# A four-layer image kernel: the last layers on other engines, the circuit made first, fewer stages ahead of the first scan steps

## The chip, the cores and the metric

The kernel runs on one core of one Trainium2 chip. A core has five engines that take their own instructions in order and wait for each other through semaphores: PE (TensorE, matmuls; its weight loads are listed as PEld), DVE (VectorE), ACT (ScalarE, table functions), POOL (GpSimd) and SP (SyncE, which here only sends DMAs). The metric is the device time of one launch in microseconds (us), the median of three runs.

## What is computed

Thirty-two images of 128 channels and 32 x 32 pixels, all in fp32, go through four layers, each added to its input after a group norm over groups of four channels:

```
x = x + conv3x3(gn(x))                       # layer 0
x = x + vmamba(gn(x))                        # layer 1: four scan directions an image
x = x + coord_attention(gn(x))               # layer 2: two scans, along rows and columns
x = x + quantum(gn(x))                       # layer 3: a 4-qubit circuit a pixel
```

The scans of layers 1 and 2 are state space models with 256 channels and 16 states: per step `h = exp(dt*A)*h + dt*u*B`, `y = sum(h*C)`. Layer 2 turns its scans into four maps an image of 32 values a channel, one of which belongs to rows and one to columns in each product:

```
result_h = sigmoid(a_h) * x_y          # rows by columns
result_w = sigmoid(a_w) * x_x          # columns by rows
out = gn(x) * conv1x1(concat(result_h, result_w))
```

Layer 3 maps each pixel to four angles (a 1x1 convolution), puts them into the state of four qubits, applies two rounds of fixed gates, measures four values and maps these to 128 channels.

## The kernel before

**Layers 0 and 1 (`images`, L873).** For each image four directions are scanned. A direction has 32 steps (two halves of channels, 16 states), each on tiles of 128 channels by 1024 pixels. Step `i` has a decay `da` on ACT (L610), an input `bu` from PE that DVE multiplies (L646, or PE transposes in 11 of 32 steps), the scan on DVE (L654), a product with `cc` on POOL (L663) and a sum in PSUM on PE (L683). `cc` is loaded by SP from `rows` in DRAM (L602), three steps ahead. 4096 such steps run one after another.

What prepares a direction is a list of small stages: `stages` (L243) has eight projections with a Silu (L263, L723), two `small` products (L282), the store of `rows`, two transposes, and the eight stages of `rates(0)`. `rates(h)` (L342) makes dt and du of one half in eight stages: `rate`, `expo`, `rounded`, `log` on PE and ACT, and then `lost`, two `whole` and `weighed` on POOL. `turns(h)` (L404) makes two transposes of du.

`Plan` (L478) puts these stages beside the scan steps by hand-written costs: a stream has a first step, a last step by which it must be done, and its stages are issued as credit on the engines allows. `Plan.alone` (L523) issues all waiting stages at once, with no scan step beside them. All this stands in a `manual_schedule` block (L1058): the order in the program is the order on each engine. Before the first step the block runs alone: layer 0 of the first image, all of the first direction's stages, transposes and second rates, and ten stages of the second direction.

**Layer 2 (`attention`, L1089)** runs two directions of 32 steps over all images together, with the same classes (`Mamba`, `Direction`, `Steps`). Its decays are also cleared at each row's start on POOL (L613). Before its first step it runs alone (L1191): the first direction's stages and both of its rates, and then ten stages of the second direction. Ahead of that it calls `circuit` (L1217), which makes from the weights of layer 3 what the last part needs: `wt` and `wb` (sixteen angle combinations), `ut` (what the circuit does to 16 sines) and `wz` (from 32 squares to 128 channels). `circuit` is some 180 small instructions on DVE with three small matmuls on PE and one sine on ACT. It stands outside the `manual_schedule` block, where the order on each engine is chosen by a scheduler that simulates the engines, oldest work first.

**The last part (`tail`, L1315)**, also ordered by the scheduler, takes one image after another: the rest of layer 2, and layer 3. For each image SP loads `xt` from DRAM (L1329). DVE makes the outer products `rh` and `rw` of the maps (L1333, L1334), PE multiplies them with `adj` (L1340, L1341), DVE normalizes `xt` (L771), multiplies by the matmul's result (L1342) and adds to `xt` (L1343). `group_stats` (L748) takes mean and variance with two small matmuls, the root on ACT (L766) and the reciprocal on DVE (L767); DVE normalizes (L771). For each half of 512 pixels a matmul `q_ps` gives 16 angles in turns (L1353), DVE takes off the whole turns in three instructions (L1354 to L1356, with `MAGIC` added and subtracted), ACT makes one sine of 16 x 1024 (L1359), PE multiplies by `ut` (L1363), ACT squares (L1364), PE multiplies by `wz` (L1368), and DVE adds the result and a bias to `xt` (L1369). POOL sends the DMA of the output (L1372). The pool `img` has three buffers for each name, so three images are on the way at most; `xn` is used twice an image.

PSUM buffers come from `mm` (two buffers) and, in the last part, `adj` and `q` (three each).

Of the kernel before, what the change touches and what calls it, by code (L numbers as in the profile page):

```python
# [43 lines left out]
def constants():  # L44
# [16 lines left out]
    small = np.zeros((16, 16 + 1 + 16 + 32))  # L61
    small[:NQ, 0:16] = turns
    small[:, 16:17] = offset
    small[:, 17:33] = start
    small[:NQ, 33:65] = ez
# [99 lines left out]
class Work:  # L165
# [10 lines left out]
    def tile(self, shape, dtype, tag, name):  # L176
        return self.pool.tile(shape, dtype, tag=tag, name=name, bufs=self.BUFS.get(tag, 1))

# [527 lines left out]
class Kernel:  # L706
# [120 lines left out]
    def run(self):  # L827
        tc, nc, d = self.tc, self.nc, self.d
        with ExitStack() as ctx:
# [25 lines left out]
            with ExitStack() as scans:  # L855
# [9 lines left out]
                self.attention(right)  # L865
# [7 lines left out]
    def images(self):  # L873
        tc, nc, d = self.tc, self.nc, self.d
        with ExitStack() as ctx:
# [182 lines left out]
            with tc.manual_schedule():  # L1058
                w = ways[0]
                plan.add(  # L1060
                    layer0(images[0]) + w.stages() + w.turns(0) + w.rates(1) + w.turns(1)
                    + ways[1].stages()[:10], 0, 0,
                )
                plan.alone()
                each = Steps.SLOTS
                for k, w in enumerate(ways):
# [12 lines left out]
                    if k + 1 < len(ways):  # L1079

                        done, b = 0 if k else 10, ways[k + 1]
                        plan.add(b.stages(at)[done:] + b.turns(0), at - 14, at + each)
                        plan.add(b.rates(1, at + 19) + b.turns(1), at + 19, at + each + 11)
# [5 lines left out]
    def attention(self, right):  # L1089
# [4 lines left out]
        with ExitStack() as ctx:  # L1094
# [13 lines left out]
            self.circuit(right, par)  # L1108
# [78 lines left out]
            with tc.manual_schedule():  # L1187
                each = Steps.SLOTS
                plan = Plan(self)
                ahead = ways[1].stages()  # L1190
                done = 5 * T // ch  # L1191
                plan.add(ways[0].stages() + ways[0].rates(1) + ahead[:done], 0, 0)
                plan.alone()
                for a, w in enumerate(ways):
# [3 lines left out]
                plan.add(ahead[done:], 1, each - 4)  # L1198
# [18 lines left out]
    def circuit(self, keep, pool):  # L1217
        nc, d = self.nc, self.d
        small = keep.tile([16, 65], F32, name="csmall")
        nc.sync.dma_start(small, d["csmall"])  # L1220
        signs, offset, start, ez = small[:NQ, 0:16], small[:, 16:17], small[:, 17:33], small[:NQ, 33:65]
# [6 lines left out]
        qw = pool.tile([16, 2 * NQ, 3], F32, name="qw")  # L1228
        nc.sync.dma_start(qw.rearrange("p a b -> p (a b)"), d["qw"].to_broadcast([16, 24]))


        self.wt = keep.tile([P, 16], F32, name="wt")
        ps = self.mm()
        nc.tensor.matmul(ps[:, :16], pre, signs, start=True, stop=True)
        nc.vector.tensor_copy(self.wt, ps[:, :16])
        self.wb = keep.tile([16, 1], F32, name="wb")
# [156 lines left out]
```

## Time and profile before

| what | us |
|---|---|
| median of three runs | 15466.06 |
| the three runs | 15443.43, 15467.32, 15466.06 |
| the profiled execution | 15464.45 |
| its span, first to last instruction | 15462.6 |
| first scan step starts | 133.65 |
| last step of layer 1 starts its scan | 14536.69 |
| first scan step of layer 2 starts | 14637.53 |
| first product of the last part starts | 14887.67 |
| mean granted clock of PE (share of full speed) | 0.915 |

The page sums all stages. Four fifths or more of the span are busy on each of PE, DVE, ACT and POOL, and nearly all of that is the 4096 steps of layer 1. The last part is 575 us, 3.7% of the span; there the engines stand quite differently, as the page's second part shows at a glance:

```profile
DVE  5888988898898889888898888989898888989787
ACT  6788888888888888888888888888888888888632
POOL 5888888888888888888888888888888888888730
PEclk8899999999999999999999999999999999999877
```

Each digit is the busy share of a fortieth of the span (387 us) in tenths, and in the last row the granted clock of PE in tenths of full speed. The last part fills the last digit and half of the one before it: POOL is nearly idle there, and PE's clock is lower.

### The profile page before, as it was taken

How to read it: one execution, taken by the hardware profiler on the slowest of the kernel's cores; microseconds unless marked ns; L12 is line 12 of the kernel's file. 1: busy time of each engine (PE TensorE's matmuls, PEld its weight loads, DVE VectorE, ACT ScalarE, POOL GpSimd, SP SyncE). 2: the span in 40 equal slices, each digit the busy share in tenths (PEclk: the TensorE clock that was granted, in tenths of full speed). 3: DMA queues.
4: the chain of work that ended last, by engine and by line, in shares of the span. 5: the costliest groups of instructions: out<-in, count | busy, mean ns of one | idle time of the engine just before them, and what ended most of it. 6: DMA issues, size and time to landing. Idle time of an engine off the chain costs nothing.

```text
span 15462.6 us, 197603 instructions
## 1 busy us (share of the span) xinstructions
PE 13209.3 (85%) x70318; PEld 8520.9 (55%) x70318; DVE 13557.1 (88%) x8999; ACT 12314.9 (80%) x21242; POOL 12569.5 (81%) x6433
## 2 busy tenths in 40 slices
PE   7888888888888888888888888888888888888776
PEld 4555555555555555555555555555555555555431
DVE  5888988898898889888898888989898888989787
ACT  6788888888888888888888888888888888888632
POOL 5888888888888888888888888888888888888730
PEclk8899999999999999999999999999999999999877
DMA  3444444444444444444444444444444444444321
GB/s 108 145 147 152 155 152 152 156 155 151 151 156 152 151 155 156 154 151 154 151 156 152 153 151 151 155 152 155 153 157 151 151 153 152 155 151 157 130 96 57
DMA packets 633029, 2277.43 MB, mean 147 GB/s; under 512 B 76808, under 2 KB 80280, under 8 KB 631912
## 3 DMA queue, kind: packets, MB, share of 16 engines
q1 hardware_dynamic: 625128, 2246.09, 42.8%
q0 software_dynamic: 4608, 16.78, 0.3%
q8 instruction: 555, 9.09, 0.2%
q14 instruction: 434, 3.56, 0.1%
q10 hardware_dynamic: 2304, 1.90, 0.0%
HBM read 2221.24 MB, written 43.25 MB: 146 GB/s over the span
## 4 chain that ended last, share of the span: by engine, by line
PE 33%; ACT 27%; DVE 22%; issue 11%; POOL 6%; DMA 1%; DVEq 0%; SPq 0%; POOLq 0%; ACTq 0%
DVE hh L654 15%; ACT da L610 8%; ACT but L639 7%; PE y L683 7%; DVE bu L646 6%; PE mm L263 6%; PE bu L624 3%; PE bu L630 3%; POOL hh L663 3%; PE mm L925 3%; PE y L679 3%; ACT L729 2%; POOL du L394 2%; PE mm L977 2%; PE mm L360 2%
## 5 line engine op out<-in xcount | busy, mean ns | idle before, releaser
L663 POOL TENSOR_TENSOR hh<-hh,cc 128x1024 f32<-128x1024 f32 x4160 | 9784.8, 2365 | 2102.5 <-DVE hh L654 1039.2
L654 DVE TENSOR_TENSOR_SCAN hh<-da,bu 128x1024 f32<-128x1024 f32 x4160 | 9413.8, 2279 | 527.6 <-PE bu L624 176.1
L610 ACT ACTIVATE da<-dt,m_na 128x1024 f32<-128x1024 f32 x4096 | 4610.1, 1143 | 591.3 <-DVE hh L654 488.9
L683 PEld LDWEIGHTS y<-cbig,hh 128*128 128x128 f32 x33280 | 3996.5, 148 | 1635.4 <-issue 1120.5
L683 PE MATMUL y<-cbig,hh 128*128 128x128 f32 x33280 | 4655.0, 286 | 147.9 <-POOL hh L663 144.3
L646 DVE TENSOR_TENSOR bu<-du,bu 128x1024 f32<-128x1024 f32 x2752 | 3330.7, 1210 | 714.2 <-PE bu L630 704.7
L639 ACT ACTIVATE but<-dut,bt 128x128 f32<-128x128 f32 x11264 | 3432.5, 391 | 0.0
L630 PE MATMUL bu<-parts,sel 48*128 48x512 bf16 x5504 | 1719.0, 394 | 649.1 <-DVE hh L654 608.2
L263 PE MATMUL mm<-hpad,m_wc 128*128 128x512 f32 x4096 | 2107.9, 639 | 2.9 <-DVE sz L446 0.8
L624 PE MATMUL bu<-cbig,but 128*128 128x128 f32 x11264 | 1639.3, 294 | 430.9 <-DVE hh L654 395.8
L624 PEld LDWEIGHTS bu<-cbig,but 128*128 128x128 f32 x11264 | 1400.5, 153 | 534.0 <-issue 321.0
L263 PEld LDWEIGHTS mm<-hpad,m_wc 128*128 128x128 f32 x4096 | 732.4, 198 | 849.5 <-issue 784.8
L679 PE MATMUL y<-m_skip,uc 128*128 128x128 f32 x4096 | 658.0, 327 | 383.1 <-ACT back L703 232.9
L630 PEld LDWEIGHTS <-sel 48*128 48x128 bf16 x5504 | 317.7, 94 | 1167.5 <-DVE hh L654 668.1
L679 PEld LDWEIGHTS y<-m_skip,uc 128*128 128x128 f32 x4096 | 613.9, 235 | 527.4 <-ACT back L703 287.6
L723 ACT ACTIVATE uc<-mm,m_pv 128x512 f32<-128x512 f32 x512 | 343.8, 686 | 377.5 <-PE mm L263 372.8
L385 POOL TENSOR_TENSOR w<-w,du 128x1024 f32<-128x1024 f32 x260 | 614.1, 2362 | 29.7 <-ACT w L378 29.7
L422 ACT COPY dut<-mm 128x512 f32<-128x512 f32 x512 | 296.5, 579 | 428.0 <-PE mm L417 425.2
L723 ACT ACT_TABLE_LOAD x482 | 618.4, 1283 | 8.6
L729 ACT ACT_TABLE_LOAD x482 | 618.4, 1283 | 8.5
L389 POOL TENSOR_TENSOR dt<-dt,relu 128x1024 f32<-128x1024 f32 x260 | 615.2, 2366 | 0.0
L394 POOL TENSOR_TENSOR du<-dt,uc 128x1024 f32<-128x1024 f32 x260 | 614.6, 2364 | 0.3
(227 smaller groups left out, 10734.5 us busy)
## 6 DMA issues: line engine op xcount, KB each, us to landing
cc<-rows SPq DMA_DIRECT2D x4160, 512.0 KB, 3.7
xt<-in_x SPq DMA_DIRECT2D x32, 512.0 KB, 4.3
x<-xt SPq DMA_DIRECT2D x32, 512.0 KB, 3.7
xt<-x SPq DMA_DIRECT2D x32, 512.0 KB, 3.5
out<-xt POOLq DMA_DIRECT2D x32, 512.0 KB, 2.9
rows<-dbl SPq DMA_DIRECT2D x130, 64.0 KB, 3.6
stats<-st SPq DMA_DIRECT2D x32, 36.0 KB, 2.3
means<-stats SPq DMA_DIRECT2D x1, 1152.0 KB, 6.3
```

Of the source, the lines that this page charges most:

```text
L263: nc.tensor.matmul(self.view(ps), m.wc[:, v, j, h * P : (h + 1) * P], self.taps(j, c), start=(j == 0), stop=(j == 3),)
L610: k.nc.scalar.activation(t, w.dt[h], AF.Exp, scale=w.m.na[:, h, n : n + 1])
L624: k.nc.tensor.matmul(t[:, b * P : (b + 1) * P], but[:, b], k.ident, start=True, stop=True, is_transpose=True,)
L630: k.nc.tensor.matmul(t[:, cs], k.sel[:, n], w.parts[:, cs], start=True, stop=True)
L639: k.nc.scalar.activation(t[:, b], w.dut[h][:, b], AF.Copy, scale=w.bt[:, b, n : n + 1])
L646: k.nc.vector.tensor_tensor(t, w.du[h], t, ALU.mult)
L654: k.nc.vector.tensor_tensor_scan(way(t), way(self.da.pop(i)), way(self.bu.pop(i)), 0.0, ALU.mult, ALU.add)
L663: k.nc.gpsimd.tensor_tensor(t, t, self.cc.pop(i), ALU.mult)
L679: nc.tensor.matmul(self.y[g][: w.bl, b], w.uc[h][:, at], m.skip[:, h], start=(b == 0), stop=False)
L683: nc.tensor.matmul(self.y[g][: w.bl, b], t[:, at], k.ident, start=False, stop=(n == DS - 1 and b == w.per - 1), is_transpose=True,)
L723: self.nc.scalar.activation(*args, AF.Silu, **kw)
L729: self.nc.scalar.preload_act_table_set("natural_log_exp_and_others")
```

## The change

The diff has four parts.

1. *The last part.* The outer products, the sum into `xt` and the root (as a power of -0.5 of variance plus 1e-5) go to POOL. Both normalizations go to ACT as `scale * x + bias`. The angles of the two halves of 512 pixels are put side by side: the first half's 16 at partitions 0 to 15, the second's at 32 to 47, so that the three steps of the sine, the sine and the Square run once on 64 partitions of 512 columns instead of on two halves or on 16 x 1024.
2. *The circuit* is made after layer 0 of the first image, inside the `manual_schedule` block, in slices of the `carry` buffer, with its values on 64 partitions instead of 16. Its four results go to DRAM and are loaded again at the start of the last part.
3. *Layer 1's first step.* Ahead of it are now issued alone the first direction's stages, its first transposes, and four of the eight stages of its second rates. The other four, the second transposes and the whole of the second direction's stages come beside the first steps.
4. *Layer 2's first step.* The same: ahead of it come the first direction's stages, eight stages of the second direction, and four stages of the second rates; the rest comes beside the first steps.

```diff
-                plan.add(
-                    layer0(images[0]) + w.stages() + w.turns(0) + w.rates(1) + w.turns(1)
-                    + ways[1].stages()[:10], 0, 0,
-                )
+                plan.add(layer0(images[0]), 0, 0)
                 plan.alone()
+                self.circuit(Slices(self.work.tile([P, 2 * HW], F32, tag="carry", name="small")))
+
+                rates = w.rates(1)
+                done = 4
+                plan.add(w.stages() + w.turns(0) + rates[:done], 0, 0)
+                plan.alone()
+                plan.add(rates[done:] + w.turns(1), 0, 11)
...
-                        done, b = 0 if k else 10, ways[k + 1]
-                        plan.add(b.stages(at)[done:] + b.turns(0), at - 14, at + each)
+                        b = ways[k + 1]
+                        plan.add(b.stages(at) + b.turns(0), at - 14, at + each)
...
-                ahead = ways[1].stages()
-                done = 5 * T // ch
-                plan.add(ways[0].stages() + ways[0].rates(1) + ahead[:done], 0, 0)
+                rates = ways[0].rates(1)
+                done = 4
+                ahead, begun = ways[1].stages(), 4 * len(chunks)
+                plan.add(ways[0].stages() + ahead[:begun] + rates[:done], 0, 0)
                 plan.alone()
+                plan.add(rates[done:], 0, 12)
...
-                plan.add(ahead[done:], 1, each - 4)
+                plan.add(ahead[begun:], 1, each - 2)
...
+        self.saved = {}
+        for name in ("wt", "wb", "wz", "ut"):
+            made = getattr(self, name)
+            self.saved[name] = self.dram.tile(list(made.shape), F32, name=name, bufs=1)
+            nc.sync.dma_start(self.saved[name], made)
...
+            mr = par.tile([P, self.n], F32, name="mr")
+            nc.vector.scalar_tensor_tensor(
+                mr, self.means[:, :, 2 * L], -1.0, self.means[:, :, 2 * L + 1], ALU.mult, ALU.mult
+            )
...
-                nc.vector.tensor_tensor(grid(rh), rows(sah), cols(xy), ALU.mult)
-                nc.vector.tensor_tensor(grid(rw), cols(saw), rows(xx), ALU.mult)
+                nc.gpsimd.tensor_tensor(grid(rh), rows(sah), cols(xy), ALU.mult)
+                nc.gpsimd.tensor_tensor(grid(rw), cols(saw), rows(xx), ALU.mult)
...
-                self.normalize(xn, xt, self.means[:, i, 2 * L :])
+                nc.scalar.activation(
+                    xn, xt, AF.Identity, bias=mr[:, i : i + 1],
+                    scale=self.means[:, i, 2 * L + 1 : 2 * L + 2],
+                )
...
-                nc.vector.tensor_tensor(xt, xt, xn, ALU.add)
-                mv = self.group_stats(xt, img)
+                nc.gpsimd.tensor_tensor(xt, xt, xn, ALU.add)
...
+                nc.vector.tensor_scalar(dv, ps[:, 0:1], 1e-5, None, ALU.add)
+                nc.gpsimd.tensor_tensor(mv[:, 1:2], dv, self.power, ALU.pow)
+                nc.vector.scalar_tensor_tensor(
+                    mv[:, 0:1], mv[:, 0:1], -1.0, mv[:, 1:2], ALU.mult, ALU.mult
+                )
...
-                self.normalize(xn, xt, mv)
...
+                nc.scalar.activation(xn, xt, AF.Identity, bias=mv[:, 0:1], scale=mv[:, 1:2])
+                kk = img.tile([64, 512], F32, tag="kk", name="kk")
+                rr = img.tile([64, 512], F32, tag="rr", name="rr")
+                sq = img.tile([64, 512], F32, tag="sq", name="sq")
+                ps = psl.tile([P, 512], F32, tag="q", name="q_ps")
+                for at, cs in halves:
+                    nc.tensor.matmul(
+                        ps[at : at + 32], wt[:, at : at + 32], xn[:, cs], start=True, stop=True
+                    )
+                nc.vector.tensor_scalar(kk, ps[:64], wb, MAGIC, ALU.add, ALU.add)
+                nc.vector.tensor_scalar(kk, kk, MAGIC, None, ALU.subtract)
+                nc.vector.scalar_tensor_tensor(rr, ps[:64], wb, kk, ALU.add, ALU.subtract)
                 nc.scalar.activation(rr, rr, AF.Sin, scale=TWO_PI)
...
+                ps = psl.tile([P, 512], F32, tag="q", name="psi_ps")
+                for at, _ in halves:
+                    nc.tensor.matmul(
+                        ps[at : at + 32], ut[at : at + 32], rr[at : at + 32], start=True, stop=True
+                    )
+                nc.scalar.activation(sq, ps[:64], AF.Square)
+                for at, cs in halves:
                     ps = psl.tile([P, 512], F32, tag="q", name="out_ps")
...
+                    nc.tensor.matmul(
+                        ps, wz[at : at + 32], sq[at : at + 32], start=True, stop=True
+                    )
```

`halves` is `[(0, first 512 columns), (32, last 512 columns)]`; `self.power` is a column of -0.5.

## The prediction

> **What bounds the kernel now.** I read the page first, then the busy time by stage, then one image of the last part in order of time, then the first 140 us and the stretch around 14600 us.
>
> ```profile
> PE 13209.3 (85%) x70318; PEld 8520.9 (55%) x70318; DVE 13557.1 (88%) x8999; ACT 12314.9 (80%) x21242; POOL 12569.5 (81%) x6433
> ```
> ```profile
> 140.00:14541.00 14401.00, 12474.97 (x68386) 8225.49 (x68384) 12858.27 (x7904) 11926.53 (x20798) 12322.59 (x6211) 0.93 0.45 153
> 14888.00:15380.00 492.00, 343.66 (x695) 105.04 (x695) 380.66 (x634) 141.77 (x169) 14.91 (x28) 0.80 0.17 61
> ```
> ```profile
> 15141.00:15158.07 17.07, 11.86 (x24) 3.58 (x24) 13.10 (x22) 5.06 (x6) 0.54 (x2) 0.80 0.18 63
> ```
>
> Columns of the stages: PE, weight loads, DVE, ACT, POOL busy, granted clock, DMA share, GB/s. The 14401 us of scan steps are not edited; only what stands ahead of them and after them moves. In the last part POOL works 15 of 492 us. One image takes 17.07 us there, 13.10 of them DVE. What holds DVE in the other 4 us is seen in one image, in order of time:
>
> ```profile
> 15141.68 1.28 ACT L766 ACT_TABLE_LOAD   x1 [3.31 <-PE mm L765]
> ...
> 15143.27 0.16 DVE L767 RECIPROCAL gn_mv<-gn_dv 128x1 f32<-128x1 f32 x1 [2.31 <-ACT gn_dv L766]
> ...
> 15144.34 3.25 PE L1353 MATMUL q_ps<-xn,wt 128*16 128x512 f32 x4 [2.74 <-DVE xn L771]
> ...
> 15147.62 0.74 DVE L1354 TENSOR_SCALAR kk<-q_ps,wb 16x512 f32<-16x512 f32 x1 [0.63 <-PE q_ps L1353]
> ...
> 15150.43 1.28 ACT L1359 ACT_TABLE_LOAD   x1 [7.19 <-DVE rr L1356]
> ...
> 15150.88 1.21 DVE L1333 TENSOR_TENSOR rh<-maps 128x1024 f32<-128x1024 f32 x1
> ...
> 15151.53 0.19 PEld L1341 LDWEIGHTS adj_ps<-rw,adj 128*128 128x128 f32 x1 [0.24 <-issue]
> 15151.96 1.02 PE L1341 MATMUL adj_ps<-rw,adj 128*128 128x512 f32 x2
> ```
>
> The brackets are idle time and what ended it: 2.31 us behind a square root that first loads its table, 0.63 and 0.54 us (the first kk) behind a matmul at half clock. Passes of 512 columns start 0.43 us apart in `adj_ps`, 0.86 apart in `q_ps`. Ahead of the scans:
>
> ```profile
> 99.73 1.13 ACT L382 ACTIVATE dt<-du,one 128x1024 f32<-128x1024 f32 x1
> ```
> ```profile
> 133.65 2.29 DVE L654 TENSOR_TENSOR_SCAN hh<-da,bu 128x1024 f32<-128x1024 f32 x1 [1.32 <-ACT da L610]
> ```
> ```profile
> 14614.83 15.84 PE L263 MATMUL mm<-means,my_wc 128*128 128x512 f32 x32 [8.01 <-ACT relu L369]
> ```
> ```profile
> 14598.10 0.42 POOL L314 TENSOR_TENSOR rest<-bt,three 128x128 f32<-128x128 f32 x1
> ```
>
> The first scan needs the decays of dt[0]; it starts 32.8 us after the last of the ACT steps that the change keeps ahead of it (100.86).
>
> [...]a switch of set costs a load[...]: 1.28 us, twice per image, for the root and the sine; the Square after the sine loads nothing. [...]L314 reads two operands as eight short rows and takes 0.42 us, less than 128 elements in proportion to the 2.36 us of 1024; so eight breaks cost nothing there. An operand with step 0, as the outer products have, no run shows.[...]
>
> **The last part, per image.**
> DVE: two products (0.69 + 0.67), statistics 1.27 + 0.20, small steps 0.15 + 0.16 + 0.22, add eps 0.16 and the new bias 0.22 (as L819 and L763), kk 0.74, subtract 0.41, rr 0.73, output 2 x 0.75: 7.1 us against 13.1. The sine's three steps run once on 64 partitions, at the price of one on 16 (512 columns either way).
> POOL: three tensor_tensors at 2.41 us (starts 83.17, 85.58, 88.00 at L389 and L394), the power 0.56 (L820), the output's DMA issue 0.53: 8.3 us against 0.5. This takes step 0 as free; bounds: 2.36 us each, as dense[...]. I take the first, because of L314.
> ACT: two normalizings at 1.24 (L912), sine 0.6 (as the Square of 512 columns), Square 0.59: 3.7 us, no table load after the first.
> PE: 8 adj, 4 q, 4 psi, 4 out passes as before, 20 x 0.43 = 8.6, plus two statistics of 0.38: 9.4 us at full clock. Half clock throughout gives 18. If q, psi and out each run their halves at once, 6 passes fall away: 6.8. I take 9.4.
> The ring of three `xt` buffers: load 3.5 (its row in the DMA table), normalizing 1.25, products 1.35, sum 2.4, statistics 1.5, PE and DVE to the variance 2.1, power 0.65, bias 0.2, normalizing 1.3, q 1.8, kk to rr 1.85, sine 0.7, psi 1.85, Square 0.65, out and its adds 2.7, issue 0.5, landing 2.9 (DMA table): 27.2 us, a third is 9.1.
> So nothing is below 9.4. Before, the image took 1.30 times its bound (17.07 / 13.10); without the root's wait of 2.31 it would be 1.13. That gives 10.6 to 12.2; I take **11.0 us**: 31 intervals x (17.07 - 11.0) = **-188 us**. Bounds 9.2 and 14.
> Added waits: the power stands in POOL's in-order queue, where a product of 2.4 us for a later image may be ahead of it, and the output's issue holds the products behind it until `xt` is final; both are in the 11.0. Five loads ahead of the first `xt` on SP (adj, wt, wb, wz, ut) put it 1.3 us later (0.33 each), hidden under the first products. After the last q the old order takes 22 us (15440.62 to 15462.6), the new about 19: q 3.6, DVE 1.85, sine 0.6, psi 3.6, Square 0.6, out 3.8 + 0.75, issue and landing 3.4 to 5.3: **-3**.
>
> **The circuit moved to the front.** Its three matmuls stand on PE between the first image's `inner` and the first projection; the second waits for the buffer that ACT frees at 50.35, so the projections start about 51.2 instead of 48.7: **+2.5 us**. The angles' sine adds a table load and a wait on ACT, over at about 54.8, where the first Silu's input is ready. DVE's 22 us of gates (14568.8 to 14592.5) end near 76; DVE is idle until the first scan, which hides them. SP sends wt, wb, wz and ut to DRAM in order, so `rows` (67.74 before) and the first `cc` wait for ut, to 77 and 79, landing by 85, and POOL needs them after the first scan. The `carry` buffer is first needed 16 steps into the scans. At 14571.0 the circuit's matmuls stood before `g8`, 1.4 us of PE with csmall's landing in front: **-1.7 us**.
>
> **Shorter ways.** In the images ACT's log of the second half ends at 100.86 + 2.5 = 103.4, the first decay at 104.5, the scan starts at 104.6 instead of 133.65: -29.0. Four POOL steps (9.6 us), two transposes and ten stages of the next direction now lie beside the first 32 steps, which took 104.9 us (32 scans counted from 133.6 to 238.5). In the next three directions, with such stages and more, 32 scans took 115.2, 124.6 and 113.8 us (the last ones bear a whole next image); over all, 32 steps take 14401 / 128 = 112.5 us. I take 110: +5. Bounds 0 and +11. Net with the circuit's delay counted: **-24**.
> In the attention PE sat idle for 8.01 us before `my_wc`. Now these projections follow the first rates: two chunks 14603.6 to 14610.5, then Silu after the log (14610.5) and a table load, two more to 14619.5, the second rates with their own table load to 14628.1, first decay 14629.2, scan 14629.5 against 14637.53: -8.0. The left-over POOL steps and two `small` stages cost about 2 in steps that run at 3.51 us on DVE (2.29 + 1.21): **-6**, with the circuit's -1.7 **-7.5**; bounds -4 and -10.
>
> **Sum.** -188 - 3 - 24 - 7.5 = -222.5 against the profiled execution's 15464.45 us (span 15462.6): 15242. The median of three runs, 15466.06, is 1.6 higher: **15244 us**.
>
> **Rivals.**
> A, the forecast, images of 10 to 12.5 us: 15213 to 15290; 50%.
> B, PE's halves overlap and the ring is the bound, 9.2 us: -244 - 34.5, 15187. For it: 6 of 20 passes[...]. Against it: 17 dependent hops between five in-order engines. 18%.
> C, the order on POOL becomes the bound: products of later images stand before the sum and the power of the older one[...]. At 13.65 us: -106 - 34.5, 15325. 27%.
> D, slower than before: step 0 makes POOL read row by row.[...] It is slower as soon as the image takes over 17.07 + 34.5 / 31 = 18.2 us, a product about 7.3 us. L314 speaks against it. 3%.
> E, images bounded by something unseen at nearly the old pace, so that the gain at the front is all: about 15435; 2%.
>
> **How the numbers follow.** A whole, half of B and half of C give 15180 to 15345, which holds about 8 in 10. A run can tell a change of about 0.2%, 31 us. A, B and C are faster by more than that: 0.95; E is no change: 0.02; D: 0.03.
>
> **What would show it.** Right: image intervals near 11 us in `xt` stores; no ACT_TABLE_LOAD between images; `rh` and `rw` on POOL at 2.4 us; DVE busy 7 of 11; first scan near 105, the attention's near 14604 (14637.5 less 24, 8 and 1.7); PEclk above 0.9 in the last part. Wrong: POOL rows for `rh` above 2.6 us; POOL idle before `rh` released by the output's adds (C); q passes 0.86 apart; a first 32 steps of 116 us or more.

## The result and the profile after

| | before | after | predicted |
|---|---|---|---|
| median, us | 15466.69 (4 runs) | 15379.16 (4 runs, 15378.28 to 15380.64) | 15244 (15180 to 15345) |
| profiled execution | 15464.45 | 15378.86 | 15242 |
| first scan step starts | 133.65 | 101.77 | 104.6 |
| first seven directions (224 steps) | 822.5 | 805.5 | 827.5 |
| other steps of layer 1, order of instructions unchanged | 13580.5 | 13572.3 | no change |
| last scan of layer 1 to first of layer 2 | 100.85 | 90.48 | 91.2 |
| 64 steps of layer 2 | 230.0 | 230.2 | 232 |
| last scan to the end (the last part) | 595.1 | 576.7 | 404 |
| granted clock of PE, whole span | 0.915 | 0.911 | |

The ratio of after to before is 0.9946 (95% interval 0.9929 to 0.9963): faster by 0.5%, not by the 1.4% that I forecast. The stages sum to -31.9 - 17.0 - 8.2 - 10.4 + 0.2 - 18.4 = -85.7 us, the difference of the two profiled executions (-85.6). The front (-31.9 - 17.0 - 10.4 + 0.2) gave -59, where the prediction had -31.5; 22 of the 28 us that it gave beyond this lie in the first seven directions. The -8.2 lies in steps whose order did not change. Of the 191 us expected in the last part, 18 came.

The page's first line, the same stages, and one image of the last part, after the change (columns as in the prediction):

```profile
PE 13201.1 (86%) x70318; PEld 8521.4 (55%) x70318; DVE 13366.8 (87%) x8776; ACT 12274.3 (80%) x21181; POOL 12786.4 (83%) x6561
```
```profile
105.00:14484.00 14379.00, 12511.47 (x68439) 8243.13 (x68438) 12857.62 (x7906) 11942.52 (x20818) 12334.36 (x6215) 0.92 0.45 153
14821.00:15300.00 479.00, 319.89 (x672) 97.04 (x672) 182.53 (x413) 99.53 (x111) 216.00 (x146) 0.70 0.17 61
15054.00:15071.07 17.07, 11.50 (x25) 3.42 (x24) 6.59 (x15) 3.59 (x4) 7.25 (x6) 0.70 0.16 61
```

The work moved as forecast: per image DVE fell from 13.10 to 6.59 us, POOL rose from 0.54 to 7.25, ACT fell from 5.06 to 3.59, and table loads in the last part fell from 64 to 1. Yet an image still takes 17.07 us, and now no engine is busy for more than 11.5 of them. Output stores begin 17.07 us apart in both kernels: the 25 intervals in the middle sum to 426.7 us before and 424.9 after. What differs is mainly the last three (60.9 and 39.5 in sum).

So one has to look for a loop of waits instead of a busy engine. Three of the longest in the view of waits of the last part (window 14900 to 15300; total us, times, longest):

```profile
POOL rh L1373 <- PE adj_ps L1382: 170.3, 24, 7.1
DVE gn_st L1388 <- POOL xt L1385: 116.5, 24, 4.9
ACT xn L1406 <- DVE gn_mv L1402: 115.0, 23, 5.0
```

Each of these comes once per image and lasts 5 to 7 us. One image in order of time, with the links that carry the loop:

```profile
15057.75 0.21 DVE L1390 BATCH_NORM_AGGREGATE gn_ag<-gn_st 128x2 f32<-128x12 f32 x1
15057.79 1.13 PE L1427 MATMUL out_ps<-sq,wz 32*128 32x512 f32 x4
...
15058.85 0.38 PE L1392 MATMUL mm<-gn_ag,cbig 128*128 128x1 f32 x2
...
15061.60 0.56 POOL L1401 TENSOR_TENSOR gn_mv<-gn_dv,power 128x1 f32<-128x1 f32 x1
15062.20 0.16 DVE L1402 SCALAR_TENSOR_TENSOR gn_mv<-gn_mv 128x1 f32<-128x1 f32 x1 [0.69 <-POOL gn_mv L1401]
15062.45 1.24 ACT L1406 ACTIVATE xn<-xt,gn_mv 128x1024 f32<-128x1024 f32 x1 [5.00 <-DVE gn_mv L1402]
...
15063.74 1.92 PE L1412 MATMUL q_ps<-xn,wt 128*32 128x512 f32 x4 [2.43 <-ACT xn L1406]
...
15065.71 0.74 DVE L1415 TENSOR_SCALAR kk<-q_ps,wb 64x512 f32<-64x512 f32 x1 [3.36 <-PE q_ps L1412]
15066.38 0.67 DVE L1384 TENSOR_TENSOR xn<-xn,adj_ps 128x512 f32<-128x512 f32 x1
...
15067.10 2.08 PE L1382 MATMUL adj_ps<-rh,adj 128*128 128x512 f32 x2 [1.44 <-DVE xn L1384]
...
15069.26 1.91 POOL L1373 TENSOR_TENSOR rh<-maps 128x1024 f32<-128x1024 f32 x1 [7.10 <-PE adj_ps L1382]
...
15071.13 2.33 POOL L1385 TENSOR_TENSOR xt<-xt,xn 128x1024 f32<-128x1024 f32 x1
```

Read on from the root of image i (L1401): its second normalizing (L1406), its angles `q_ps`, its `kk`, and only then, behind `kk` in DVE's queue, the multiply of image i+1 (L1384). The multiply frees a PSUM buffer for an `adj` matmul of a later image, that one frees the buffer into which POOL writes a product `rh`, and the sum of image i+1 (L1385) stands behind this product on POOL. After it come that image's statistics, mean, variance, root: the loop is closed, once per image. Little of it overlaps with the next image, because each queue holds the next image's instruction behind this image's.

The first three lines, one image earlier, show that a second path runs beside this one and is a little longer. The statistics are done at 15057.96 (`gn_ag`), but the mean (L1392) starts only at 15058.85, when PE is through with `out` (L1427). So the path over POOL has 0.9 us to spare, and the mean waits for PE's queue; what stands in it is seen below, in the experiment that moves the sum.

At the front the mechanism is the forecast one. The last log and the first decay now stand right ahead of the first scan, and the projections `my_wc` start at 14543.5 instead of 14614.8 (57 us of that from the earlier end of layer 1):

```profile
99.56 1.13 ACT L399 ACTIVATE dt<-du,one 128x1024 f32<-128x1024 f32 x1
100.60 5.29 ACT L627 ACTIVATE da<-dt,m_na 128x1024 f32<-128x1024 f32 x5
101.77 2.29 DVE L671 TENSOR_TENSOR_SCAN hh<-da,bu 128x1024 f32<-128x1024 f32 x1 [4.50 <-ACT da L627]
```
```profile
14543.51 16.29 PE L280 MATMUL mm<-means,my_wc 128*128 128x512 f32 x32
```

### The profile page after: what moved, and what is told of

It reads as the page before. It is cut to its first block, busy times and chain, and to the rows that moved or that the text cites. A ratio compares the mean times of both kernels' runs of the same rounds, so it can differ in the third digit from the quotient of the medians.

```text
span 15377.0 us, 197657 instructions
## 1 busy us (share of the span) xinstructions
PE 13201.1 (86%) x70318; PEld 8521.4 (55%) x70318; DVE 13366.8 (87%) x8776; ACT 12274.3 (80%) x21181; POOL 12786.4 (83%) x6561
## 5 line engine op out<-in xcount | busy, mean ns | idle before, releaser
L406 POOL TENSOR_TENSOR dt<-dt,w 128x1024 f32<-128x1024 f32 x260 | 615.3, 2367 | 0.2
```

What stands on the lines that cost most here:

```text
L406: nc.gpsimd.tensor_tensor(self.dt[h], self.dt[h], t[name], op)
```

## The experiments

"Interval" is the time between the starts of two output stores in the middle of the last part; "tail" runs from the last scan to the end. Eight of the changed kernels ran once, and not all on the same chip; the kernel before took 15435 to 15467 us beside them (medians, the lowest a single run). The tail is a better measure than the total: the unchanged steps of layer 1 vary from 13541 to 13581 us between the profiles. The tail varies too: nearly the same last part took 595.1 and 602.4 us in the first two rows. In the traces of the kernels before and after PE's clock is granted at full or at half speed, and each of the 862 and 872 stretches at one of these, but for the last, which the end of the trace cuts off, lasts a whole multiple of 3.413 us (1 to 29 of them; in the kernel after, 15004.92 to 15011.75 is at 1.00 and 15011.75 to 15021.99 at 0.50); these 3.413 us are the window of PE's clock that the texts below count in.

| kernel | total, us | tail | interval | clock in the tail |
|---|---|---|---|---|
| before | 15466.69 | 595.1 | 17.07 | 0.78 |
| front alone | 15404.77 | 602.4 | 17.07 to 18.07 | 0.76 |
| front, root on POOL | 15414.27 | 605.5 | 17.24 to 18.69 | 0.69 |
| after | 15379.16 | 576.7 | 17.07 | 0.70 |
| after, five buffers | 15381.91 | 579.6 | 17.07 | 0.70 |
| after, products on DVE | 15366.80 | 573.2 | 17.07 | 0.70 |
| after, more PE work | 15440.81 | 647.4 | 20.48 | 0.79 |
| after's order, sum first | 15381.48 | 584.9 | 17.07 | 0.69 |
| after's order, multiply first | 15285.12 | 509.9 | 14.2 to 14.9 | 0.73 |
| after's order, both first | 15256.96 | 483.1 | 13.65 | 0.74 |
| hand-written order | 15265.63 | 460.3 | 12.2 to 13.6 | 0.75 |
| the same, operands from PSUM | 15187.12 | 385.4 | 9.9 to 11.2 | 0.80 |
| second order, operands from PSUM | 15167.55 | 360.2 | 10.4, and 8.74 | 0.85 |
| after, circuit late | 15372.53 | 576.5 | 17.07 | 0.70 |

**The front alone.** Before's last part behind after's front:

```diff
-                nc.gpsimd.tensor_tensor(grid(rh), rows(sah), cols(xy), ALU.mult)
+                nc.vector.tensor_tensor(grid(rh), rows(sah), cols(xy), ALU.mult)
...
-                nc.gpsimd.tensor_tensor(xt, xt, xn, ALU.add)
+                nc.vector.tensor_tensor(xt, xt, xn, ALU.add)
+                mv = self.group_stats(xt, img)
...
```

> The change without its last part: images are finished as before (products, sum and normalizing on DVE, root on ACT, sines of both halves one after the other), while the circuit, the first steps of layer 1 and of layer 2 are as changed. Theory: the front gives nearly all of the gain (first scan 31.9 us earlier, first seven directions 17, the way into layer 2 10.4), so about 15466 - 65 = 15400, and images 17.07 us apart. Rival (the new last part gave the gain, the front little): within 20 us of 15466.

The ratio to before was 0.997 (0.9958 to 0.9982), 47 us between the medians on that chip. That is more than half of the 87.5 us that the whole change gained on its own chip. The intervals were 17.07 us for the most part, up to 18.07 in the middle.

**Five buffers.** The ring of `xt` was one of the forecast's bounds (9.1 us).

```diff
-            img = ctx.enter_context(tc.tile_pool(name="img3", bufs=3))
+            img = ctx.enter_context(tc.tile_pool(name="img3", bufs=5))
```

> The changed kernel with five buffers instead of three for each name in the last part. Rival theory (ring of three xt buffers bounds the image, as in the prediction's sum of 27 us over three): images come down to 27 / 5, so to PE's or POOL's bound, 8 to 11 us, and the whole by some 200 us. Theory (one image's first half hangs on the previous image's through the order on the engines, buffers are free): images stay at or near 17.07 us unless the order changes with the buffers.

The interval stayed 17.07: the ring is not what holds it. Near the end three stores were 15.27 to 15.28 us apart; the kernel after shows one such interval too. The expectations below take this for the loop at full clock. It isn't: the granted clock was 0.78 in these intervals, and they stand where POOL has no product left ahead of the sum. Nor were the first intervals of the kernel before (15.77 us) at full clock; it was 0.73 and 0.82 there. No run here shows the loop of the kernel after at full clock.

**Products on DVE.** POOL's order was rival C.

```diff
-                nc.gpsimd.tensor_tensor(grid(rh), rows(sah), cols(xy), ALU.mult)
-                nc.gpsimd.tensor_tensor(grid(rw), cols(saw), rows(xx), ALU.mult)
+                nc.vector.tensor_tensor(grid(rh), rows(sah), cols(xy), ALU.mult)
+                nc.vector.tensor_tensor(grid(rw), cols(saw), rows(xx), ALU.mult)
```

> The kernel after with one edit: the two outer products of each image on DVE, as before the change (0.69 + 0.67 us there), instead of POOL (1.91 + 1.91 us). The order of all other instructions on each engine stays. Theory 'order on POOL': the product ahead of the sum in POOL's queue costs the loop about 3.1 us; with it gone the loop needs about 12.3 us at full clock, below 4 windows of 13.65, so intervals of 13.65 us, 31 x 3.41 = -106 us, about 15275 us. Rival 'another order is worse': DVE has the products where it is short of nothing, but the loop still goes through adj at half clock, kk behind q and norm behind norm, and intervals stay 17.07 us: about 15380 us.

17.07 again, as the rival said, with 3.8 us less on POOL. The timeline shows what replaced the product ahead of the sum:

```profile
15056.18 2.34 POOL L1385 TENSOR_TENSOR xt<-xt,xn 128x1024 f32<-128x1024 f32 x1 [5.96 <-DVE xn L1384]
...
15057.29 2.33 DVE L1373 TENSOR_TENSOR rh<-maps 128x1024 f32<-128x1024 f32 x1 [0.57 <-PE adj_ps L1382]
15059.53 1.27 DVE L1388 BATCH_NORM_STATS2 gn_st<-xt 128x6 f32<-128x512 f32 x2
```

Now the product stands ahead of the statistics on DVE, and beside POOL's sum it takes 2.33 us instead of the 1.21 of the kernel before (the expectation named 0.69, which is the price of a multiply over half the columns). So this run doesn't decide on POOL's order.

**The root alone.** Of the last part's changes only this one, behind the new front:

```diff
-        nc.scalar.activation(dv, ps[:, 0:1], AF.Sqrt, bias=self.eps)
-        nc.vector.reciprocal(mv[:, 1:2], dv)
+        nc.vector.tensor_scalar(dv, ps[:, 0:1], 1e-5, None, ALU.add)
+        nc.gpsimd.tensor_tensor(mv[:, 1:2], dv, self.power, ALU.pow)
```

> The last part of the kernel before (products, sum, normalizing on DVE, halves one after the other) behind the front of the kernel after, with one edit: the root of the group norm on POOL (add eps on DVE, power on POOL) in place of ACT's square root and DVE's reciprocal. That takes two table loads of 1.28 us per image away (the sine's table stays in) and most of the 2.31 us for which DVE waited. Theory 'whole windows': without the wait the loop needs about 15.77 (the first intervals of the kernel before, with PE at full clock) - 1.9 = 13.9 us, which is over 4 windows (13.65), so it is drawn out to 17.07 again and the tail stays within 10 us of the 602 us of the front alone: about 15400 us. Rival 'the wait counts': intervals of 14 to 15.2 us, 31 x (17.07 - 14.6) = -77 us, about 15330 us.

```profile
15054.00:15071.07 17.07, 13.78 (x25) 4.23 (x24) 13.16 (x22) 2.23 (x3) 0.98 (x2) 0.70 0.17 61
```

Two table loads and a wait of 2.31 us per image went, and the interval did not shorten. PE's busy time per image rose from 11.86 to 13.78 us, its clock in the tail fell from 0.76 to 0.69. The intervals, most often 17.24 or 17.25, are close to five clock windows but not exactly on them. The tail is what the theory of whole windows said; its sum started from the 15.77 that was not at full clock, and the scheduler also put two `adj` matmuls of an image behind `out`, so what the root alone is worth stays open.

**More work for PE.** Four extra matmuls of 384 columns, whose results nothing reads, ahead of each of the two statistics matmuls, to see whether the clock rises with PE's work:

```diff
+                for _ in range(4):
+                    nc.tensor.matmul(
+                        ps[:, 8:392], adj[:, 0], self.maps[:, 0:3], start=True, stop=True
+                    )
                 nc.tensor.matmul(ps[:, 0:1], self.group, ag[:, 0:1], start=True, stop=True)
```

> The changed kernel with four extra matmuls of 384 columns ahead of each of the two statistics matmuls of an image; their results are not used. They only keep PE busy in its idle time. Theory (the image's time is pinned to five windows of PE's clock, 17.07 us, by stretches at half clock): granted clock near 1.0 in the last part and images 13 to 15.5 us apart although PE has more to do, some 50 to 110 us off the whole. Rival (the order's chain is 17 us whatever the clock): 17 us or more, slower by the extra matmuls that fall on the chain.

The clock in the tail rose from 0.70 to 0.79, not to 1. While it was full, two intervals were 14.4 us; then they settled at 20.48 us, 10.24 of each at full and 10.24 at half clock. The forecast of this run failed, but it shows a second place where the interval stands still: the trace grants the clock in multiples of 3.413 us, and 17.07 and 20.48 are five and six of these. With the extra matmuls the scheduler chose another order too (the multiply stands ahead of `kk`), so the run doesn't separate the clock from the order.

**The order by hand.** The instructions of the last part unchanged, four buffers, their order written out:

```diff
+            order = [
+                (angles, -1), (times(0), 0), (times(1), 0), (turns, -1), (total, 0), (sine, -1),
+                (adjust(0), 1), (sums, 0), (product("rh"), 2), (state, -1), (square, -1), (mean, 0),
+                (spread, 0), (variance, 0), (eps, 0), (root, 0), (shift, 0), (normal, 1), (again, 0),
+                (result, -1), (added, -1), (adjust(1), 1), (product("rw"), 2), (store, -1), (load, 3),
+            ]
+            with tc.manual_schedule():
```

Each entry is a step and the image it belongs to, counted from the turn's own; `times` is the multiply, `total` the sum.

> The changed kernel with the same instructions in the last part in an order written by hand (second half of image i beside the first half of image i+1, products two images ahead, sum ahead of products on POOL) and four buffers. Theory (order on the engines, not any engine's work, makes the 17.07 us): images about 10 us apart, at most 11.5, the whole 15379 - 31 x 7 = about 15160. Rival (the clock's windows pin the image): 10.24, 13.65 or 17.07 us, with half clock in each image. Rival (an engine's work or waiting for semaphores is the bound): 15 us or more.

The tail fell by 116 us; the ratio to before is 0.9879 (0.9863 to 0.9896). The fourth buffer is no rival, since five brought nothing: the same instructions in another order gave part of what the engines' busy times promised. The expected 10 us was missed (it was about 13.1), and two DVE steps in its timeline show a part of the reason:

```profile
15044.47 1.90 POOL L1385 TENSOR_TENSOR rw<-maps 128x1024 f32<-128x1024 f32 x1
15044.53 1.86 DVE L1443 SCALAR_TENSOR_TENSOR gn_mv<-gn_mv 128x1 f32<-128x1 f32 x1 [0.67 <-POOL gn_mv L1439]
...
15050.24 2.33 POOL L1411 TENSOR_TENSOR xt<-xt,xn 128x1024 f32<-128x1024 f32 x1 [1.36 <-DVE xn L1407]
...
15051.18 1.68 DVE L1464 TENSOR_SCALAR kk<-kk 64x512 f32<-64x512 f32 x1
```

A step on 128 values takes 1.86 us instead of 0.16, and the subtract 1.68 instead of 0.41; each ends just after the POOL instruction that was there first (by 0.02 and 0.29 us).

**Which place in the order.** Three kernels take after's own order, written out (in the middle images it is the scheduler's, instruction by instruction on each engine), with one move or both:

```diff
-                (angles, -1), (turn(0), -1), (times(0), 0), (turn(1), -1), (times(1), 0), (turn(2), -1),
-                (adjust(1, 0), 1), (adjust(1, 1), 1), (sine, -1), (rh, 4), (early, 2), (total, 0),
+                (angles, -1), (turn(0), -1), (turn(1), -1), (turn(2), -1),
+                (adjust(1, 0), 1), (adjust(1, 1), 1), (sine, -1), (early, 2), (total, 0), (rh, 4),
...
-                (again, 0), (normal, 1), (load, 2),
+                (normal, 1), (times(0), 1), (times(1), 1), (again, 0), (load, 2),
```

This is both; "sum first" moves `rh` behind `total` alone, "multiply first" moves `normal` and `times` alone.

> The last part of the kernel after, with its own instructions and its own order on every engine written out by hand, and one move: on POOL the sum of an image stands ahead of the product rh of the image four later, not behind it. In the kernel after the sum begins 3.1 us after its multiply is done. Theory 'one-image loop in the queues': the loop is 15.28 us at full clock (the intervals where it ran free) and loses 2.9 us: about 12.4, drawn out to 4 windows: intervals of 13.65 us, the last part 31 x 3.41 = 106 us shorter than the 577 us of the kernel after, about 470 us, in all about 15275 us. Rival 'POOL's order is not on the loop' (the products on DVE left 17.07): intervals of 17.07, about 15380 us.

> As the run before it, but the other move alone: the first normalizing of the next image stands ahead of the second one of this image on ACT, and its two multiplies ahead of this image's kk, subtract and rr on DVE; on POOL rh stands ahead of the sum as in the kernel after. Theory 'one-image loop in the queues': the multiply no longer waits for q and kk, but the sum still stands behind rh, rh behind the adj matmul of the second half and that behind q: of the loop only kk and the multiplies (about 1.5 us) go: intervals between 13.65 and 17.07, if whole windows hold 17.07 again, the last part 560 to 580 us. Rival 'the multiply alone sets it': 12 to 13.65 us, the last part 420 to 475 us.

> Both moves together: the next image's multiplies ahead of kk, and the sum ahead of rh on POOL. Theory 'one-image loop in the queues': the loop through norm, q, adj and rh is open; left is sum 2.33, statistics 1.5, out and its adds about 2.5, mean to variance 1.1, root and bias 0.8, norm 1.24, multiplies 1.3: 10.8 us, at half clock in parts 11 to 13; the last part 400 to 455 us, in all 15200 to 15260 us. Rival 'an engine or the clock is the bound, not the order': intervals stay over 13.65 and the last part over 475 us.

The sum first alone brought nothing: its forecast of 13.65 us failed, and 17.07 stayed. In its trace the sum follows the multiply at once and the statistics end at 15066.3, but then the mean waits on PE until 15070.20:

```profile
15060.67 0.67 DVE L1408 TENSOR_TENSOR xn<-xn,adj_ps 128x512 f32<-128x512 f32 x1
...
15061.39 2.07 PE L1401 MATMUL adj_ps<-rh,adj 128*128 128x512 f32 x2 [1.44 <-DVE xn L1408]
...
15063.25 1.91 PE L1401 MATMUL adj_ps<-rw,adj 128*128 128x512 f32 x2
...
15064.96 1.91 PE L1401 MATMUL adj_ps<-rh,adj 128*128 128x512 f32 x2
15066.10 0.21 DVE L1419 BATCH_NORM_AGGREGATE gn_ag<-gn_st 128x2 f32<-128x12 f32 x1
...
15066.81 1.35 PE L1481 MATMUL psi_ps<-rr,ut 32*32 32x512 f32 x4
...
15069.15 1.13 PE L1492 MATMUL out_ps<-sq,wz 32*128 32x512 f32 x4
15070.20 0.38 PE L1423 MATMUL mm<-gn_ag,cbig 128*128 128x1 f32 x2
```

This is the second path from the multiply to the mean, over PE: the `adj` matmuls wait for the PSUM buffer that the multiply frees, run at half clock, `psi`, the Square and `out` stand behind them, and the mean stands behind `out`. It takes as long here as in the kernel after, so the sum could not shorten the loop. Both paths start at the multiply, and moving that one earlier shortens both: 14.5 us, within the expected 13.65 to 17.07, but with a tail of 510 us, not 560 to 580. With both moves the interval is 13.65 us (13.64 to 13.66 in 25 intervals on end), equal to four clock windows. That is over the 11 to 13 us of the forecast, and the tail of 483 lies where the rival had it (over 475), so more than these two places holds that loop. The tail is 94 us shorter than in the kernel after, with not one instruction of the last part other than there; the total of 15257 is 122 us below its median, but 31 us of this are unchanged steps of layer 1.

**Operands from PSUM.** The hand-written order, with the two DVE steps that were long beside POOL's instructions changed: the bias reads the mean from PSUM, and the subtract is one step with the one after it, which reads `q` from PSUM. The deviation reads the mean from PSUM too (not shown here), its copy falls away, and `wb2` is `wb` times 2 pi:

```diff
-                    mv[:, 0:1], mv[:, 0:1], -1.0, mv[:, 1:2], ALU.mult, ALU.mult
+                    mv[:, 0:1], t["ps1"][:, 0:1], mv[:, 1:2], -1.0, ALU.mult, ALU.mult
...
-                nc.vector.tensor_scalar(kk, kk, MAGIC, None, ALU.subtract)
-                nc.vector.scalar_tensor_tensor(t["rr"], t["q"][:64], wb, kk, ALU.add, ALU.subtract)
+                nc.vector.scalar_tensor_tensor(
+                    t["rr"], kk, MAGIC, t["q"][:64], ALU.subtract, ALU.subtract
+                )
...
-                nc.scalar.activation(t["rr"], t["rr"], AF.Sin, scale=TWO_PI)
+                nc.scalar.activation(t["rr"], t["rr"], AF.Sin, bias=wb2, scale=-TWO_PI)
```

> The hand-written order as it stands, with three small DVE steps made so that they do not read two operands from SBUF or copy SBUF to SBUF: the new bias takes the mean from PSUM (tensor_scalar), the deviation too (the copy falls away), and the sine's argument is (kk - MAGIC) - q with the sine's own scale and bias in place of a subtract and a second add: one DVE step of 0.41 us less. Theory[...]: the steps that took 1.58 to 1.68 us and 1.86 us beside POOL's instructions cost 0 and about 0.16; the loop loses 1.7 us at the bias (it stands between the root and the second normalizing) and up to 1.6 at kk: intervals 13.1 -> 10.5 to 11.5 us, about 15265 - 31 x 2.1 = 15200 us. Rival 'only the record is long': the loop is set by adj at half clock and by the order, and intervals stay at 12.7 to 13.1: 15255 us or more.

The same step in its timeline, again beside `rw`:

```profile
15045.78 1.90 POOL L1387 TENSOR_TENSOR rw<-maps 128x1024 f32<-128x1024 f32 x1
15045.83 0.22 DVE L1444 TENSOR_SCALAR gn_mv<-mm,gn_mv 128x1 f32<-128x1 f32 x1 [0.68 <-POOL gn_mv L1440]
```

0.22 instead of 1.86 us; the interval fell from about 13.1 to 10.6 and the tail by 75 us, a ratio to before of 0.9822 (0.9806 to 0.9839). In the order by hand, too, a step that read PSUM kept its length beside POOL: `rr` took 0.74 us beside `rh`. The statistics did so as well (1.27 us for two beside `rh`), though they read only SBUF. What holds the long steps up is not shown: with the operand the form of the instruction changed too. A part of the 75 us is the step and the copy that fell away (0.41 and 0.16 us an image, some 18 us in all at most).

**A second order.** As the last one, with five buffers and the list

```diff
+                (total, 0), (store, -2), (adjust(0), 1), (turns, -1), (sine, -1), (product("rh"), 2),
+                (sums, 0), (state, -1), (square, -1), (mean, 0), (spread, 0), (variance, 0),
+                (normal, 1), (eps, 0), (root, 0), (shift, 0), (adjust(1), 1), (times(0), 1),
+                (times(1), 1), (again, 0), (result, -1), (added, -1), (angles, 0),
+                (product("rw"), 2), (load, 4),
```

> As the run before it (bias and deviation from PSUM, sine's argument with one DVE step less) and a second hand-written order: the multiplies by adj of the next image before the last adds of this one, adj of the second half ahead of out, angles of an image at the end of its own turn, the store one image later, the second product after the root with nothing of DVE behind it, five buffers instead of four. Worked out from the measured durations: DVE 1.35 + 1.47 + 1.47 + 0.9 + 1.4 = 6.6, POOL 2.33 + 2.08 + 0.56 + 1.9 + 0.6 = 7.5, and the path from one sum to the next (sum 2.4, statistics 1.6, mean and variance 2.0, root and bias 0.8, two multiplies 1.4) 8.2 us. Theory[...]: intervals of 8.6 to 10 us, 31 x (13.1 - 9.5) = -112 us against the hand-written order, about 15155 us. Rival 'PE at half clock holds it': intervals stay over 11 us: 15200 us or more.

Intervals are 10.4 us where PE falls to half clock for one window in three, and 8.74 where it doesn't; only the second kind lies in the forecast's 8.6 to 10. A stretch of that kind, all at full clock:

```profile
15110.00:15118.73 8.73, 7.51 (x26) 2.45 (x26) 6.17 (x14) 3.28 (x4) 6.58 (x5) 1.00 0.30 111
```

PE is busy for 7.51 of 8.73 us; here an engine is nearly the bound. The total, 15167.55 (15153.20 to 15185.00, 4 runs), is 0.9817 of before (0.9802 to 0.9831). It beats the kernels before and after by far; from the order before it (0.9822) the ratio doesn't separate it, though its tail was 25 us shorter in the one profile of each.

**The circuit late.** One part of the front undone:

```diff
-                self.circuit(Slices(self.work.tile([P, 2 * HW], F32, tag="carry", name="small")))
...
+            self.circuit(par)
             view = lambda ps: ps.rearrange("p (n l) -> p n l", l=S)
```

> The kernel after with one part of the change undone: the circuit is prepared at the head of the attention part again, where the kernel before had it, and not at the front. The shorter ways stay. Theory of the prediction: the circuit's matmuls delayed the first projections by 2.5 us and its place in the attention cost 1.7 us: the first scan is 2.5 us earlier than the kernel after (101.8 to 105.1 over its runs), about 99 to 102, the stretch from the last scan of layer 1 to the first of layer 2 about 92.2 instead of 90.5, and the first seven directions stay at 805.5. Rival 'the circuit's work at the front is what moved the seven directions': these go back towards 822.

The first scan starts at 100.82; the twelve profiles with the circuit at the front have 101.73 to 105.09, median 103.2. So the circuit costs about 2.4 us at the front, near the forecast 2.5, but with one run against that spread the size is rough. The way into layer 2 is 97.0 us, against a forecast of 92.2, and against 90.4 to 90.6 in nine of the twelve and 93.9 to 94.1 in the other three. This run doesn't put the circuit quite where the kernel before had it: its first matmul starts 26.4 us after the last scan, not 34.3, and the projections behind it start at 38.5 us, in the kernel before at 35.7, in the kernel after at 33.1. From before to after, then, the circuit's move brought some 2.6 us of this way, and the rest, 7.8, is the shorter way. The seven directions took 808.0: their shorter time belongs to the shorter ways, not to the circuit.

## Why the prediction was wrong

**The step that failed** is in "The last part, per image": "Before, the image took 1.30 times its bound (17.07 / 13.10); without the root's wait of 2.31 it would be 1.13. That gives 10.6 to 12.2; I take 11.0 us", and with it the term -188. The middle intervals didn't change at all. The factor was taken from a stage in which DVE was busy for 13.10 of 17.07 us and carried over to one in which DVE has 6.6, POOL 7.3 and PE 9.4 at full clock, as if the waits shrank with the work. What bounds the image in their place is the path through the queues from one image's multiply to the next one's: 17.07 us, with PE at half clock on parts of it. The scheduler's order fixes it, and this path I never added up for the new order: the prediction's own list of one image from load to landing, 27.2 us, was divided by the three buffers, as if three images could overlap wherever the ring lets them. The experiments show it from two sides. More buffers and 3.8 us less on POOL don't move the interval; two moves in the order bring 94 us of tail without touching an instruction.

**Clock.** The forecast counted on a clock above 0.9 in the last part, which was an estimate of mine that no run had shown (in the kernel before it was 0.80 there); it was 0.70. What that costs is an estimate: on the path over POOL `q_ps` takes 1.92 us and the first `adj` pair 2.08, and 1.05 and 1.02 in the full-clock images of the run with more PE work (the same in the second order's stretch at clock 1.00). Together with the 0.9 us to spare this gives 17.07 - 0.9 - 1.9, about 14 us at full clock (the path over PE, with three `adj` pairs, would be shorter). By this estimate about half of the 6 us between 11.0 and 17.07 is the order and half the clock.

The interval of 17.07 us is the same number before and after, and in both it is five windows of 3.413 us: before 10.24 us at full and 6.83 at half clock, after 6.83 and 10.24. Intervals that stand at whole numbers of windows, 13.65, 17.07 and 20.48 us, are what these runs show. So that two kernels with different work show the same interval is in part a matter of where the loop settled. Why it settles, and why the loops of 14.5, 13.1 and 10.6 us don't, was not tested.

**Rivals.** E, "images bounded by something unseen at nearly the old pace", with 2%, was what happened in the last part. The total is 56 us below its 15435: the front gave some 28 us more than forecast, the last part 18, and the unchanged steps 8. C had the right kind (products ahead of the sum), at 13.65 us, but its place was only one of two parallel paths, as the sum first shows. B: that the halves overlap on PE was a guess of mine, and they do (in the second order four `psi` passes take 1.05 us at full clock, not 4 x 0.43), which is part of why PE needs 7.5 us and not 9.4 in the image at full clock; but the ring never became the bound. D fell: that POOL reads row by row was a guess which no trace had shown, and the products take 1.91 and 1.90 us, far below D's 7.3. The chances don't add up to the range either: A, half of B and half of C are 72.5 in 100, not 8 in 10.

**Prices.** POOL's `rh` and `rw` take 1.91 and 1.90 us, less than the dense sum's 2.33; I had 2.41. L314 hadn't shown that: its 0.42 us for 128 elements is more, not less, than an eighth of 2.36 us (0.30). POOL's 7.25, DVE's 6.59 and ACT's 3.59 us per image stand against 8.3, 7.1 and 3.7. What I left out is the price of DVE's steps beside POOL's instructions. It didn't hold the middle images of the kernel after, where the two steps fell in POOL's pauses (0.16 and 0.41 us; near the end, beside the sum, the subtract took 2.07), but cost the hand-written order 1.7 and 1.2 us per image in lengthened steps. The end of the last part was costed at -3; the last three intervals alone gave -21.

**The front** was right in mechanism for the two first scans and had one term at nothing. First scan -31.9 against -29.0; over the profiles with this front the median is 103.2, so -30.4. The +5 for the first 32 steps was +1.2 (106.2 against 105.0), and the prediction ended its count there. But the new streams of stages change the order on the engines up to the seventh direction, and directions two to seven went from 717.5 to 699.3 us: the second got slower (115.2 to 129.0), the later ones quicker (the fifth 120.1 to 107.6). Which of the moved stages does this, no run tells. The way into layer 2 gave -10.4 ahead of the scan, where the prediction had -9.7 (-8.0 and -1.7; the traces give about -7.8 and -2.6), and +0.2 in place of +2 in the steps.

## What to carry to other kernels

Work taken off the busiest engine pays only until the longest path through the in-order queues from one iteration to the next becomes the bound: write down which instruction of iteration i stands ahead of which of iteration i+1 on each engine, and add up that loop, before you scale a busy time. Look for parallel paths, too: a part that brings nothing alone may still be needed for the next (the sum first brought nothing by itself, and 27 us of tail on top of the multiply first). When such a loop binds, look at the clock as well: in these runs intervals of four, five and six windows (13.65, 17.07 and 20.48 us) stood still from image to image. And when steps go to POOL, look at the DVE steps on the path beside them: here one with all its operands in SBUF took 1.86 us instead of 0.16, a subtract from SBUF to SBUF 1.58 to 1.68 instead of 0.41, and the first only 0.22 once it read the mean from PSUM.

## What was not expected of the hardware

- Intervals that stand at 13.65, 17.07 and 20.48 us: 17.07 in two kernels with different work, 20.48 in a kernel whose images had come 14.4 us apart while the clock was full.
- Outer products with step-0 operands on POOL in 1.91 us, dense tensors of the same size in 2.33.
- A DVE step on 128 values that took 1.86 us beside a POOL instruction of 1.90, and 0.22 when one operand was in PSUM.
